# Two graph attention layers on one core: masks cleared ahead of their readers, counts last in a round

## The chip, the cores and the metric

The kernel runs on one core of a Trainium2 chip. The core has five engines that each work through a queue of their own, in order: TensorE (PE in the profile, with PEld for its weight loads), VectorE (DVE), ScalarE (ACT), GpSimd (POOL) and SyncE (SP). [...] The metric is the device time of one execution in microseconds. A measurement here is a median of several runs.

## What is computed

There are N = 3327 nodes with D = 1024 features each, and an adjacency matrix of 3327 x 3327 integers. Each pair is drawn with a chance of 0.0024 in either direction, the matrix is made symmetric, and every node is its own neighbour; a row then holds 17.1 ones on average. Two layers follow one another. Both are graph attention with a residual and a layer norm; layer 0 has 8 heads of 128 features, layer 1 has one head and a ReLU.

```python
# layer 0
h = (x @ W).reshape(C, H, D)
e = alpha_src[:, :, None] + alpha_dst[:, None, :]      # per head
e = jnp.where(e >= 0, e, NEG_SLOPE * e)
e = jnp.where(adj[None] == 0, -jnp.inf, e)
attn = jax.nn.softmax(e, axis=-1)
out = jnp.einsum('hij,hjd->hid', attn, h_heads)
x = _layernorm(x + out)
# layer 1: the same with one head, relu(attention @ h), and again a layer norm
```

## The kernel before

**Tiles and stages.** The nodes form 26 tiles of 128 rows (`NT`); the last one has 127. The program has three parts. The projection stage multiplies every tile of x with the weights of layer 0 on TensorE (`project`, line 538: a tile has three column groups c of 347, 347 and 346 columns, each a chain of 8 products in float32), writes h to memory (`keep`), and beside this makes the neighbour lists of all tiles. From tile 13 on it also sums the early half of the lists (`sums_so_far`, line 617; one small step of it at each pace call). Then one of two arms runs both layers: `sparse` (line 955), which gathers the listed rows of h by indirect DMA, or `by_pairs` (line 1373), which goes over all 26 x 26 pairs of tiles.

**Which arm runs** is decided on the chip. A tile's list holds, for each group of 32 rows and each half of the columns, 256 places (`HG2`); what does not fit goes to one more block of 128 places for the whole tile. `words` counts the neighbours of each row in each half, `ends` takes running sums of the counts within groups of 32 rows and keeps what lies over 256, and `ends2` takes the running sum of that over the tile, into `cnt[:, t, 3]`. A node's own entry is no part of the list: it is cleared from the mask first, and added from the diagonal later. At the end of the stage the largest of these numbers is compared with 128, and the result is read as the branch's condition:

```python
        nc.vector.tensor_copy(big[:, :, 1], cnt[:, :, 3])                                   # L900
        nc.vector.tensor_scalar(flag, most, float(P), None, op0=OP.is_gt)                   # L907
    with tc.If(dense > 0) as arm:                                                           # L1491
        with ExitStack() as own:
            by_pairs(own)
    with arm.Else():
        with ExitStack() as own:
            sparse(own)
```

**Masks.** A tile's 128 rows of the adjacency matrix are loaded from memory as bytes by a DMA that GpSimd issues (`load_mask`, line 524). There are three buffers, and tile t uses number t % 3 (line 526). `words` (line 335) has its own entry cleared by GpSimd (line 342), counts each half with two ScalarE instructions (line 346), and folds the mask into words with three VectorE instructions (line 353). `count(t)` (line 566) calls `words(t)` and then `load_mask(t + 2)`.

**The list work** is a generator, `listing` (line 572). A round has eight steps and serves two tiles, `new` = t + 1 (its entries are found) and `old` = t (its lists are put together on TensorE by `give` and read by `take` and `sources`). The steps of a round before the change: four with `keys` and `columns` on VectorE (with `ends(t + 3)` in the second and `ends2(t + 3)` in the fourth), then `take`, `ways` and `count(t + 4)`, then `sources`, then `places`, then `spread`.

**The order** is written out by hand (`tc.manual_schedule`), so each engine's queue is the order in which the Python code runs. `pace` (line 608) is called after every second product; it advances `listing` until its steps done are in proportion to the calls: `done * slots[1] >= slots[0] * 216`. `slots` starts at a number set by hand. Rounds for tiles 0 to 2 are partly written out before the loop (`count(0)` to `count(2)`, `ends`, `ends2`); the loop over t = 3 to 25 then holds two projections of tile t, one of t + 1, and the transposes of tile t + 2 (`flip`: four on TensorE into the one bank "T", copied out by ScalarE at line 199).

**The arm `by_pairs`** has no order by hand. For each tile it loads the adjacency rows again, from memory into one buffer `ad` in bfloat16, compares them with zero (line 1387), turns the 26 blocks on TensorE (line 1393), copies them to bytes and stores them. Layer 0 then takes 7 chunks of up to four tiles, 8 heads and 26 source tiles j: ScalarE forms e of 128 x 512 (Relu), VectorE adds and multiplies with the mask, and TensorE makes two products of it, of 128 x 512 with h (line 1448) and of 32 x 512 with a column of ones (line 1450). After each head the sums are copied, turned and added. `project1` (line 1401) makes 16 products of 128 x 512 for each tile, and layer 1 makes, for each of 26 tiles and 26 sources, three products of 341 or 342 columns (line 1485). It reads neither the lists nor the masks of the first stage.

Of the kernel before, what the change touches and what calls it, by code (L numbers as in the profile page):

```python
# [14 lines left out]
OP = mybir.AluOpType  # L15
# [4 lines left out]
P = 128  # L20
# [6 lines left out]
def kernel(  # L27
# [28 lines left out]
    nc = tc.nc  # L56
    N, D = x.shape
    H, DH = a0_src.shape
    NT = (N + P - 1) // P
# [35 lines left out]
    def rows(t):  # L95
        return min(P, N - t * P)
# [217 lines left out]
    class Edges:  # L314
# [10 lines left out]
        def factors(self):  # L325
# [6 lines left out]
            nc.gpsimd.tensor_copy(mv[:, 1, :], r[:, 1, :])  # L332
            nc.gpsimd.tensor_tensor(mv[:, 2, :], r[:, 1, :], mv[:, 1, :], OP.subtract)

        def words(self, ad, junk):

            sbuf, ph, t = self.ph.sbuf, self.ph, self.t  # L340
            own = ad[:, t * P : (t + 1) * P].bitcast(mybir.dt.int8)
            nc.gpsimd.affine_select(  # L342
                out=own, in_=own, pattern=[[1, P]], compare_op=OP.not_equal, fill=0.0, base=0, channel_multiplier=-1
            )
            for n in range(2):
                nc.scalar.activation(junk, ad[:, n * THR : (n + 1) * THR], AF.Copy, accum_out=self.d[:, n : n + 1])  # L346
            self.deg_b = sbuf("deg_b", [P, 2], 4, dt=BF16)
            nc.scalar.activation(self.deg_b, self.d, AF.Copy)
            w = ad.bitcast(I32)
            for n in range(3):  # L350
                m = WD >> n
                half = sbuf(f"wd{n}", [P, m], 4 if n == 2 else 1, dt=I32)
                nc.vector.scalar_tensor_tensor(
                    half, w[:, m:], 1 << n, w[:, :m], op0=OP.logical_shift_left, op1=OP.bitwise_or
                )
                w = half
            self.bytes = w.bitcast(U8)
# [152 lines left out]
    with ExitStack() as own, tc.manual_schedule():  # L510
        ph = Phase(own, "proj", {"A": 2, "T": 1})
# [4 lines left out]
        xts, xT, ads, hts, accs = {}, {}, {}, {}, {}  # L516
        lists = [Edges(ph, t) for t in range(NT)]
# [15 lines left out]
        def flip(t, g, who=None):  # L533
            if g == 0:
                xT[t] = ph.sbuf("xT", [P, KT, P], 2) if t else part.sbuf("z", [P, KT, P], 1, "xT")
            (who or ph).turned(xT[t], xts[t] if g == 0 else xts.pop(t), g)

        def project(t, c, paced=True, between=None):

            acc = accs[t, c] = bank("A", [P, CUTS0[c + 1] - CUTS0[c]], "mm")  # L540
            for k in range(KT):
                nc.tensor.matmul(  # L542
                    acc, xT[t][:, k, :], wt[:, k, CUTS0[c] : CUTS0[c + 1]], start=k == 0, stop=k == KT - 1
                )
                if k == 3 and between:
                    between()
                if paced and k % 2 == 1:
                    pace()

        def keep(t, c):  # L550
            if t not in hts:
                hts[t] = ph.sbuf("ht", [P, HW0], 3)
            ht, acc, c0 = hts[t], accs.pop((t, c)), CUTS0[c]
            m = min(CUTS0[c + 1], D) - c0
            if c == 2:
                nc.scalar.activation(sd0[:, t].rearrange("p a h -> p (a h)"), acc[:, m:], AF.Copy)
                lists[t].factors()
                nc.scalar.activation(ht[:, D : D + H], acc[:, m + H :], AF.Exp)
                nc.scalar.activation(ht[:, D + H :], acc[:, m + H :], AF.Exp, scale=SLOPE)
                scored.add(t)  # L560
            nc.scalar.activation(ht[:, c0 : c0 + m], acc[:, :m], AF.Copy)  # L561
            kept[t] = kept.get(t, 0) + 1
            if kept[t] == 3:
                nc.sync.dma_start(h0_d[t * P : (t + 1) * P, :HW0], hts.pop(t))

        def count(t):
            if t < NT:
                lists[t].words(ads.pop(t), junk)
                if t:
                    load_mask(t + 2)  # L570

        def listing():

            for t in range(-1, NT):
                old, new = lists[t] if t >= 0 else None, lists[t + 1] if t + 1 < NT else None
                for s in range(4):
                    if old and s:
                        old.give(s - 1)
                    if new:
                        (new.keys, new.columns)[s // 2](s % 2)  # L580
                    if s == 1 and 2 < t + 3 < NT:
                        lists[t + 3].ends(tri_b)
                    if s == 3 and 2 < t + 3 < NT:
                        lists[t + 3].ends2(all_b)
                    yield
                if old:
                    old.give(EB - 1)
                    old.give(EB)
                    old.take()
                if new:  # L590
                    new.ways()
                count(t + 4)
                yield
                if old:
                    old.sources()
                    yield
                while new and t + 1 not in scored:
                    yield
                if new:
                    new.places()  # L600
                    yield
                    new.spread()
                    yield

        scored, kept, soon = set(), {}, []
        steps, slots, done = listing(), [0, 0], [0]

        def pace():
# [202 lines left out]
        for g in range(NG):  # L811
            nc.vector.memset(tri[g * GT : (g + 1) * GT, g * GT : (g + 1) * GT], 1.0)
        nc.gpsimd.affine_select(
            out=tri, in_=tri, pattern=[[1, P]], compare_op=OP.is_ge, fill=0.0, base=0, channel_multiplier=-1
        )
        tri_b = pool.tile([P, P], BF16, bufs=1, name="tri_b")
# [6 lines left out]
        )  # L823
        all_b = pool.tile([P, P], BF16, bufs=1, name="all_b")
        nc.vector.tensor_copy(all_b, tri)
        count(0)
        for _ in range(2):
            next(steps)
# [8 lines left out]
        project(1, 2, False)  # L837
        keep(1, 2)
        lists[0].ends2(all_b)
        lists[1].ends(tri_b)  # L840
        flip(3, 0)
        load_x(5)
        count(2)

        done[0], slots[:] = 4, [9, (NT - 3) * 12 + 13]
        project(2, 2, True, lambda: flip(3, 1))
        keep(2, 2)
        flip(4, 0)
        lists[1].ends2(all_b)
        lists[2].ends(tri_b)  # L850
        project(3, 2, True, lambda: flip(4, 1))
        keep(3, 2)
        lists[2].ends2(all_b)
        for t in range(3, NT):
            load_x(t + 3)
            if 4 <= t < 4 + KT:
                nc.sync.dma_start(wt1[:, t - 4, :], w1[(t - 4) * P : (t - 3) * P, :])
            if t == 12:
                n, own_a = NT - 1, pool.tile([P, NT], I32, bufs=1, name="own")
                nc.vector.memset(own_a[:, n:], 0)  # L860
                step, m = adj.ap[0][0] + 1, rows(n)
                nc.sync.dma_start(
                    own_a[:, :n], bass.AP(tensor=adj.tensor, offset=adj.offset, ap=[[step, P], [P * step, n]])
                )
                nc.sync.dma_start(
                    own_a[:m, n:], bass.AP(tensor=adj.tensor, offset=adj.offset + n * P * step, ap=[[step, m], [1, 1]])
                )
            if t == 11:
                ph.iota([P, P], [[1, P]], "io_t", base=1, dst=io_t)
                same = ident[: NG * H, : NG * H].rearrange("p (g h) -> p g h", g=NG)  # L870
                met = meets.rearrange("p (g t) -> p g t", g=NG)
                nc.vector.tensor_reduce(met[:, :, 0], same, AX.X, OP.max)
                nc.vector.tensor_copy(met[:, :, 1:], met[:, :, :1].to_broadcast([NG * H, NG, GT - 1]))
                nc.vector.tensor_reduce(heads, same.rearrange("p g h -> p h g"), AX.X, OP.max)
            if t == 16:
                nc.gpsimd.tensor_copy(loop, own_a)
            if t in (9, 10):
                table, w = (h0_d, HW0) if t == 9 else (y_d, HW)
                blank = pool.tile([P, 1, HP - w], F32, bufs=1, name=f"blank{t}")
                nc.gpsimd.memset(blank, 0.0)  # L880
                nc.sync.dma_start(
                    table[:, w:].rearrange("(t p) w -> p t w", p=P), blank.to_broadcast([P, NT, HP - w])
                )
            if t == NTH:
                soon.append(sums_so_far())
            for c in (0, 1):
                project(t, c)
                keep(t, c)
            if t + 2 < NT:
                flip(t + 2, 0)  # L890
            if t + 1 < NT:
                project(t + 1, 2)
                keep(t + 1, 2)
            if t + 2 < NT:
                flip(t + 2, 1)
# [624 lines left out]
```

## Time and profile before

| what | number |
| --- | --- |
| median of 3 runs | 1940.33 us (1933.4 to 1942.73) |
| the profiled execution | 1945.79 us |
| its span, first to last instruction | 1944.1 us |
| busy: PE, DVE, ACT, POOL | 1633.7, 1184.5, 573.4, 1092.2 us |
| projection stage: first and last product of line 542 | 13.0 and 570.5 us |
| the flag is written (line 907) | 571.5 us |
| first instruction of the arm that ran (`sparse`) | 594.2 us |
| products of line 1267 (layer 1's projection, in `sparse`) | 1230.8 to 1935.4 us |

Times in the profile's rows are microseconds from the span's start; a duration printed as "mean ns" is in nanoseconds. A row of a timeline has the start, the length, the engine, the line, the operation, and how many instructions were merged into it; in square brackets is the time the engine stood idle before it and what ended that. A float32 product appears as two records, so 8 records are 4 products. The arm that ran is `sparse`; `by_pairs` has no row in this profile.

### The profile page before, as it was taken

To read this page: it belongs to the slowest core of one execution; us is meant where nothing else is said; L and a number is where in the kernel's file an instruction comes from. 1 tells how busy PE (TensorE), PEld (TensorE's weight loads), DVE (VectorE), ACT (ScalarE), POOL (GpSimd) and SP (SyncE) were. 2 spreads that over 40 slices of the span, in tenths; PEclk is the share of its full clock that TensorE was granted. 3 is DMA by queue.
4 is the path that set the end of the run, shared out by engine and by line. 5 is a ranking of instruction groups with operands and counts; after the bars stand their busy time and mean duration, and the time that the engine had idled before them with its cause. 6 is when DMAs were issued, how large, how long until landed. Compare 5 with 4: busy or idle time off the path is not lost.

```text
span 1944.1 us, 35431 instructions
## 1 busy us (share of the span) xinstructions
PE 1633.7 (84%) x13168; PEld 919.9 (47%) x13168; DVE 1184.5 (61%) x3261; ACT 573.4 (29%) x1565; POOL 1092.2 (56%) x1580
## 2 busy tenths in 40 slices
PE   8699989989994777777777665798989999899988
PEld 5466556655563554554455442243434434333433
DVE  6699988777765776777777774243444344434342
ACT  5656554444321222222222121022122221222121
POOL 4433346656555666666666555565656666565640
PEclk9899999999996878888878877899999999999999
DMA  6555779887779999999999998899999999899980
GB/s 178 91 130 114 144 152 293 255 249 238 247 271 349 381 391 393 383 393 371 402 386 386 374 313 301 310 374 340 346 350 369 335 394 342 331 362 340 325 302 33
DMA packets 183364, 585.16 MB, mean 301 GB/s; under 512 B 36168, under 2 KB 42824, under 8 KB 183182
## 3 DMA queue, kind: packets, MB, share of 16 engines
q0 software_dynamic: 131056, 457.74, 68.4%
q1 hardware_dynamic: 52126, 125.06, 17.2%
q8 instruction: 107, 1.75, 0.4%
q14 instruction: 75, 0.61, 0.1%
HBM read 586.09 MB, written 51.22 MB: 328 GB/s over the span
## 4 chain that ended last, share of the span: by engine, by line
PE 43%; issue 10%; DVE 6%; ACT 4%; DMA 4%; POOL 1%; another core or an unknown queue 0%; DVEq 0%; ACTq 0%; POOLq 0%
PE mm L1267 17%; PE acc L1235 13%; PE acc L1129 8%; PE acc L1110 2%; DMA src<-h_d,idx 2%; PE tr L196 1%; ACT L1193 1%; PE acc L1118 1%; DVE e L1098 1%; ACT own L1076 1%; DMA near<-h_d,idx 1%; DVE pr L982 1%; DVE st L217 1%; ACT L220 1%; DMA src<-y_d,idx 1%
## 5 line engine op out<-in xcount | busy, mean ns | idle before, releaser
L542 PE MATMUL mm<-wt,xT 128*128 128x347 f32 (+1 forms) x1248 | 416.6, 475 | 6.8 <-ACT ht L561 3.3
L1267 PE MATMUL mm<-wt,xT 128*128 128x512 f32 x832 | 395.5, 613 | 2.6 <-issue 2.3
L1017 POOL DMA_INDIRECT src<-y_d,idx x248 | 249.1, 1005 | 166.8 <-PE acc L1235 71.0
L542 PEld LDWEIGHTS mm<-wt,xT 128*128 128x128 f32 x1248 | 228.5, 195 | 118.3 <-issue 19.7
L1017 POOL DMA_INDIRECT src<-h_d,idx x184 | 196.5, 1068 | 121.3 <-PE acc L1129 35.8
L1267 PEld LDWEIGHTS mm<-wt,xT 128*128 128x128 f32 x832 | 152.3, 193 | 211.5 <-issue 206.7
L1270 DVE SCALAR_TENSOR_TENSOR o<-mm,y 128x512 f32<-128x512 f32 x52 | 36.0, 692 | 322.2 <-PE acc L1235 126.4
L1017 POOL DMA_INDIRECT near<-y_d,idx x168 | 169.5, 1009 | 108.7 <-PE acc L1235 48.3
L1129 PE MATMUL acc<-src,e 128*32 128x128 f32 x2944 | 161.3, 324 | 52.1 <-issue 47.5
L1017 POOL DMA_INDIRECT near<-h_d,idx x120 | 130.6, 1088 | 82.4 <-PE acc L1129 31.0
L1235 PE MATMUL acc<-src,es 128*32 128x341 f32 x1488 | 130.6, 485 | 41.8 <-DVE es L1226 31.8
L1129 PEld LDWEIGHTS acc<-src,e 128*32 128x32 f32 x2944 | 111.5, 130 | 113.4 <-issue 93.8
L1098 DVE TENSOR_TENSOR e<-oh,way 128x1024 f32<-128x1024 f32 x104 | 127.1, 1222 | 59.3 <-ACT w L1096 43.1
L1129 PE MATMUL acc<-near,e 128*32 128x128 f32 x2048 | 116.0, 333 | 48.7 <-issue 34.8
L199 ACT ACTIVATE xT<-tr 128x512 f32<-128x512 f32 x104 | 62.1, 598 | 299.9 <-PE tr L196 151.6
L1129 PEld LDWEIGHTS acc<-near,e 128*32 128x32 f32 x2048 | 79.7, 133 | 93.7 <-issue 84.4
L1096 ACT ACTIVATE w<-way 128x32 f32<-128x32 f32 x104 | 20.3, 195 | 351.4 <-DVE way L1094 186.6
L1249 ACT ACTIVATE z<-y,ri 128x342 f32<-128x342 f32 (+1 forms) x78 | 39.5, 569 | 277.0 <-issue 121.6
L1235 PE MATMUL acc<-near,es 128*32 128x342 f32 (+1 forms) x1008 | 85.8, 469 | 21.3 <-DVE es L1226 14.0
L629 POOL DMA_INDIRECT near<-h_d,idx x76 | 82.1, 1080 | 31.5 <-issue 22.9
L1235 PEld LDWEIGHTS acc<-src,es 128*32 128x32 f32 x1488 | 44.4, 114 | 115.0 <-issue 61.1
L346 ACT ACTIVATE junk<-ad 128x1664 uint8<-128x1664 uint8 x52 | 83.8, 1611 | 16.2 <-POOL ad L342 14.8
(242 smaller groups left out, 2587.8 us busy)
## 6 DMA issues: line engine op xcount, KB each, us to landing
h_d<-ht SPq DMA_DIRECT2D x26, 520.0 KB
own<-h_d SPq DMA_DIRECT2D x26, 520.0 KB
y_d<-y SPq DMA_DIRECT2D x26, 514.0 KB
y<-y_d SPq DMA_DIRECT2D x26, 514.0 KB
x<-in_x_dram SPq DMA_DIRECT2D x25, 512.0 KB
y<-in_x_dram SPq DMA_DIRECT2D x25, 512.0 KB
out_dram<-o SPq DMA_DIRECT2D x25, 512.0 KB
ad<-in_adj_dram POOLq DMA_DIRECT2D x25, 415.9 KB
```

The lines of the kernel that those rows point to most:

```text
L199: nc.scalar.activation(part, tr, AF.Copy)
L346: nc.scalar.activation(junk, ad[:, n * THR : (n + 1) * THR], AF.Copy, accum_out=self.d[:, n : n + 1])
L542: nc.tensor.matmul(acc, xT[t][:, k, :], wt[:, k, CUTS0[c] : CUTS0[c + 1]], start=k == 0, stop=k == KT - 1)
L629: nc.gpsimd.indirect_dma_start(out=src[n % 3][:, g, :], out_offset=None, in_=h0_d[:THR, :], in_offset=bass.IndirectOffsetOnAxis(ap=idx[:, ...
L1017: nc.gpsimd.indirect_dma_start(out=s[:, g, :w], out_offset=None, in_=table[:n, :], in_offset=bass.IndirectOffsetOnAxis(ap=idx[:, t, b * NG ...
L1098: nc.vector.tensor_tensor(e, oh.unsqueeze(2).to_broadcast([P, ng, H, wide]), wp.unsqueeze(3).to_broadcast([P, ng, H, wide]), OP.mult,)
L1110: nc.tensor.matmul(self.acc[j - 1].rearrange("p h d -> p (h d)"), ident, self.h[:, (j - 1) * HALF : j * HALF], start=False, stop=False,)
L1129: nc.tensor.matmul(self.acc[h // 4][g * GT : (g + 1) * GT, h % 4, :], e[:, g, h, :], rowsof[:, g, h, :], start=first and h % 4 == 0, stop= ...
L1235: nc.tensor.matmul(self.acc[c][to, :m], es[:, g, :], s[:, g, CUTS[c] : CUTS[c + 1]], start=b == 0, stop=b == EB,)
L1249: nc.scalar.activation(z[:, cut], self.res[:, cut], AF.Copy, scale=ri[:, 1:2])
L1267: nc.tensor.matmul(acc, xT[:, k, :], wt1[:, k, half], start=k == 0, stop=k == KT - 1)
L1270: nc.vector.scalar_tensor_tensor(o[:, half], acc, 0.0, res[:, half], op0=OP.max, op1=OP.add)
```

## The change

Four things change, all in the first stage. `words` no longer clears the mask; a new `clear` does, and is called for tiles 0 to 2 ahead of everything and for tile t + 4 in the third step of round t. `count(t + 4)` moves from the fifth step of a round to a last step of its own, and `places` and `spread` become one step, so a round still has eight. Ahead of the loop, `slots` starts at 4 of 284 instead of 9 of 289; `lists[1].ends` comes after the transposes of tile 3; and `count(2)` and `lists[1].ends2` come after the first paced projection, `project(2, 2)`. One projection of tile 3 moves from the loop to a place ahead of it, between `lists[2].ends` and `lists[2].ends2`.

```diff
+        def clear(self, ad):
+            own = ad[:, self.t * P : (self.t + 1) * P].bitcast(mybir.dt.int8)
+            nc.gpsimd.affine_select(
+                out=own, in_=own, pattern=[[1, P]], compare_op=OP.not_equal, fill=0.0, base=0, channel_multiplier=-1
+            )
         def words(self, ad, junk):
-            own = ad[:, t * P : (t + 1) * P].bitcast(mybir.dt.int8)
-            nc.gpsimd.affine_select(
...
+        def clear(t):
+            if t < NT and t not in cleared:
+                cleared.add(t)
+                lists[t].clear(ads[t])
         def count(t):
             if t < NT:
+                clear(t)
                 lists[t].words(ads.pop(t), junk)
                 if t:
                     load_mask(t + 2)
@@ listing
+                    if s == 2 and t >= 0:
+                        clear(t + 4)
...
                 if new:
                     new.ways()
-                count(t + 4)
                 yield
...
                 if new:
                     new.places()
-                    yield
                     new.spread()
                     yield
+                count(t + 4)
+                yield
@@ ahead of the loop
+        for t in range(3):
+            clear(t)
         count(0)
...
         lists[0].ends2(all_b)
-        lists[1].ends(tri_b)
         flip(3, 0)
         load_x(5)
-        count(2)
-        done[0], slots[:] = 4, [9, (NT - 3) * 12 + 13]
+        lists[1].ends(tri_b)
+        done[0], slots[:] = 4, [4, (NT - 3) * 12 + 8]
         project(2, 2, True, lambda: flip(3, 1))
         keep(2, 2)
+        lists[1].ends2(all_b)
+        count(2)
         flip(4, 0)
-        lists[1].ends2(all_b)
-        lists[2].ends(tri_b)
         project(3, 2, True, lambda: flip(4, 1))
         keep(3, 2)
+        lists[2].ends(tri_b)
+        project(3, 0)
+        keep(3, 0)
         lists[2].ends2(all_b)
@@ loop
-            for c in (0, 1):
+            for c in (0, 1)[t == 3 :]:
                 project(t, c)
```

More of the change, by code (lines that the diff above doesn't have):

```diff
@@ L333, in factors @@
             nc.gpsimd.tensor_tensor(mv[:, 2, :], r[:, 1, :], mv[:, 1, :], OP.subtract)
-        def words(self, ad, junk):
-            sbuf, ph, t = self.ph.sbuf, self.ph, self.t
-            own = ad[:, t * P : (t + 1) * P].bitcast(mybir.dt.int8)
+        def clear(self, ad):
+            own = ad[:, self.t * P : (self.t + 1) * P].bitcast(mybir.dt.int8)
             nc.gpsimd.affine_select(
@@ L344, in words @@
             )
+        def words(self, ad, junk):
+            sbuf = self.ph.sbuf
             for n in range(2):
@@ L600, in listing @@
                     new.places()
-                    yield
                     new.spread()
                     yield
-        scored, kept, soon = set(), {}, []
+                count(t + 4)
+                yield
+        scored, cleared, kept, soon = set(), set(), {}, []
         steps, slots, done = listing(), [0, 0], [0]
```

## The prediction

> **What bounds the kernel now.** I read the stage boundaries first, then the waits of the stage that the change touches. In VectorE's timeline the flag that selects the arm is written at 571 us, and the arm's first instruction runs at 594 us:
>
> ```profile
> 571.46 0.14 DVE L907 TENSOR_SCALAR flag<-most 1x1 int32<-1x1 f32 x1
> 594.24 0.12 DVE L965 MEMSET y<- 128x4 f32 x3 [6.06 <-DMA half_d<-z]
> ```
>
> So everything the edit moves lies in the first 30% of the span. There TensorE is the nearly full engine. Its timeline shows the gaps that the change aims at (line 362 waits behind ScalarE, which waits for a clear; line 466 waits for `spread`), and what a gap costs afterwards: eight records of line 542 take 4.18 us after a gap, where the same eight took 2.57 us at 87.93.
>
> ```profile
> 64.14 0.16 PE L362 MATMUL dd<-deg_b,tri_b 128*128 128x2 bf16 x1 [4.52 <-ACT cnt L388]
> 64.24 0.63 PE L196 MATMUL tr<-ident,x 128*128 128x128 f32 x4
> 64.70 4.18 PE L542 MATMUL mm<-wt,xT 128*128 128x346 f32 x8
> 78.66 0.48 PE L466 MATMUL xp<-mvg,place 128*128 128x168 bf16 x3 [9.34 <-ACT mvg L447]
> 79.01 3.98 PE L542 MATMUL mm<-wt,xT 128*128 128x346 f32 x8
> ```
>
> The table of waits up to 600 us (total, times, longest) shows the other target, VectorE waiting for the clear:
>
> ```profile
> DVE wd L353 <- POOL ad L342: 57.0, 13, 6.9
> ```
>
> **The change, part by part: first, which arm runs.** This decides everything, and it is a matter of order, not of duration. Before, `count(2)` stood ahead of `project(2, 2)`. Now it stands behind, and `project(2, 2)` makes four pace calls, with slots 5, 6, 7, 8 of 284. After 4 steps done, the condition 4 x 284 < 6 x 216 releases step 5 (`ways`), 5 x 284 < 7 x 216 step 6 (`places`, `spread`), and 6 x 284 = 1704 < 8 x 216 = 1728 step 7, the round's new last step: `count(3)`. `count(3)` ends with `load_mask(5)`, and 5 % 3 = 2: that is tile 2's buffer, which `count(2)` has not read yet. The queues of the built program agree: ScalarE has tile 3's two counts ahead of tile 2's, and tile 2's wait for the fifth mask load issued, tile 5's. So tile 2's list is made of tile 5's rows; that is the part of the computation which changes. Tile 2's clear ran on the old contents, and tile 5's comes a round later, so these rows are counted with their own entries.
>
> I summed the reference's adjacency matrix as `words`, `ends` and `ends2` do. With cleared masks the number compared with 128 is between 5 and 115 over the 26 tiles (tile 5: 47). Tile 5's rows uncleared gain 32 entries in the first half of each group: groups of 301, 294, 282 and 294 against 256 places give 147, and 10 + 12 from the second half make 169. 169 > 128, the flag is 1, and `by_pairs` runs both layers over all pairs. It has no row in this profile, so it is built up from the nearest rows.
>
> *A, up to the arm.* Removed: gaps of 4.52 + 9.34 us, another of 0.88 at 84.5, and 1.6 + 1.4 us of slow products after them: -17.7. Added: tile 2's counts wait for the new load. A mask load issued at 90.40 keeps the DMA engines busy until about 97.5 (share 0.94, then 0.20): 7.1 us.
>
> ```profile
> 91.00:97.00 6.00, 6.00 (x25) 3.80 (x24) 5.66 (x19) 5.70 (x17) 2.03 (x9) 1.00 0.94 149
> 97.00:98.00 1.00, 1.00 (x8) 0.59 (x6) 0.97 (x2) 0.00 (x0) 0.84 (x5) 1.00 0.20 20
> ```
>
> Tile 3's load is issued at 59.3 and lands at 66.4; its clear takes 0.3; tile 5's load then lands at 73.8; the two counts take 3.6 (59.62 to 63.2 before), to 77.4. Behind them in ScalarE's queue is the copy of tile 4's first transposes (0.6), and TensorE's second transposes of tile 4 need that bank. TensorE gets there at about 69.1 and waits until 78.0, 8.9 us, plus 1.6 slow: +10.5. Later TensorE waits behind VectorE's late clears (releasers of lines 435, 447 and 650 between 350 and 500 us: 4.83 + 2.33 + 1.73 + 0.99 + 0.65 + 0.54): -11.1. The clears' DMAs lead by 11 steps instead of 16, over 20 us against 7.1. Counts late in the round leave line 362 two steps instead of five; ScalarE's 3.6 us fit in two steps of about 1.9 us only just, so this gain can vanish. Arm at 594 - 17.7 + 10.5 - 11.1 = 576 (565 to 605: more hidden, or no gain at all).
>
> *B, loading the masks again*, one buffer, so a chain per tile: 7.1 load + 2.6 compare (line 224's 0.812 us for 1024 elements, times 3328/1024) + 4.0 until the last transposes (eight at 0.15, two copies of 1024 from PSUM at twice line 1270's 0.692) + 0.3 handed over = 14.0; 26 x 14.0 = 364. Ends: 11.5 (compare and copies at half) and 18 (the load writes two bytes instead of one): 300 to 470.
>
> *C, layer 0.* The rows for the two products of 512 columns, for ScalarE's 128 x 512 and for VectorE's:
>
> ```profile
> 1714.47 3.70 PE L1267 MATMUL mm<-wt,xT 128*128 128x512 f32 x8
> 1718.01 1.89 PE L1235 MATMUL acc<-end,es 128*128 128x341 f32 x6
> 1719.73 3.60 PE L1267 MATMUL mm<-wt,xT 128*128 128x512 f32 x8
> 1723.26 1.93 PE L1235 MATMUL acc<-src,es 128*32 128x341 f32 x24
> L199 ACT ACTIVATE xT<-tr 128x512 f32<-128x512 f32 x104 | 62.1, 598 | 299.9 <-PE tr L196 151.6
> L1270 DVE SCALAR_TENSOR_TENSOR o<-mm,y 128x512 f32<-128x512 f32 x52 | 36.0, 692 | 322.2 <-PE acc L1235 126.4
> ```
>
> Four products go from 1714.47 to 1718.01: 0.885 us each. Two of them per source, 1.77 us, exceed ScalarE's 0.60 and VectorE's 0.69, so TensorE sets the pace: 52 x 0.885 = 46.0 per head. At a head's end a chain stands open: two copies 1.2, transposes of the sums 0.6, of the next row 0.6, Exp 0.6, Relu 0.6, mask 0.7, handovers 0.4, together 4.7, and 1.6 of slow products after it as above: 52.3. 48 heads x 52.3 = 2510; the last chunk has half the width, 8 x 28.8 = 230; layer norms hold VectorE up 2 us in each chunk, 14. Sum 2754. Ends: 0.86 per product and no open chain, 44.7 x 48 + 22.4 x 8 = 2325; the mean of line 1267 over its busy time, 395.5/416 = 0.95, and a chain of 10 us, 3120.
>
> [...]
>
> *D, `project1`:* 16 x 0.885 + eight transposes 1.2 + a copy 0.6 + 0.1 = 16.1, x 26 = 419 (390 without the transposes and half the copy; 500 with the 3 us of scoring in series).
> *E, layer 1:* six records of line 1235 take 1.72 us up to the next row, 0.573 per product; 78 x 0.573 + 0.4 = 45.1, x 26 = 1173 (1160 to 1250). ScalarE and VectorE have a quarter of C's width against 1.72 us.
> *F, tail:* norm and store, 10.
>
> Sum: 576 + 364 + 2754 + 419 + 1173 + 10 = 5296, and 1.7 around the span: 5298. The profiled execution is 5 us above the median, less than this sum can tell; I take **5300 us**.
>
> **The rivals.** *The list arm still runs.* For it: the edits remove real gaps, as costed. Against it: the queue order and 169 > 128. It decides if tile 2's number stays at 128 or below. Time: 1945.8 - 17.7 + 10.5 - 11.1 = 1927, faster by 0.7% than the median. Chance 0.05. *The 32-column products cost next to nothing in `by_pairs`.* For it: 24 records of 128 x 32 take 1.93 us, hardly more than six of 128 x 128. Against it: those go in fours to different columns, here each stands alone between two full ones. Time: layer 0 falls to 48 x (23.0 + 6.3) + 8 x 17.3 + 14 = 1559, total 4103. Chance 0.07. *ScalarE, VectorE and TensorE take turns* because e is too scarce: 0.6 + 0.69 + 1.77 + 0.3 = 3.4 per source, layer 0 at 48 x 95 + 8 x 51 = 4970, total 7500. Against it: e has four buffers. Chance 0.06.
>
> **How the numbers follow.** The forecast, `by_pairs` bound by TensorE, has 0.80; 0.02 is left for others. The ends of A to F add up to 4750 and 5955 if all fall on one side; 4850 to 5850 leaves their corners and the rivals out, about 0.2. A measurement of this kernel can tell 0.5% from no change. Faster 0.05 (the first rival), same 0.01, slower 0.94.
>
> **What would show it.** Rows of `by_pairs` at all, and none of `sparse`; tile 2's counts on ScalarE behind tile 3's, with an idle time ended by a DMA; some 7.1 us or more from load to load in B; pairs of 512-column products 1.77 us apart with a gap near 5 us every 26 pairs. The forecast falls if the profile has line 1129's successor in it.

## The result, and the profile after

The changed kernel takes 5737.44 us (median of 6 runs, 5734.51 to 5743.24), the kernel before 1941.53 us on the same chip (6 runs, 1927.85 to 1953.39). The ratio is 2.957, with a 95% interval of 2.945 to 2.970: slower. The profiled execution has a span of 5741.5 us.

The page of the changed kernel shows which arm ran. First the shares of the chain that ended last by engine, then the costliest groups (busy us and mean ns of one; idle time before it and what ended that):

```profile
PE 85%; DVE 6%; DMA 5%; ACT 3%; issue 1%; POOL 0%; SPq 0%; another core or an unknown queue 0%; DVEq 0%; POOLq 0%; ACTq 0%
L1458 ACT ACTIVATE e<-R,nb,a 128x512 f32<-128x512 f32 (+1 forms) x1456 | 1120.7, 780 | 1881.5 <-PE sum L1465 1879.6
L1459 DVE SCALAR_TENSOR_TENSOR e<-e,b,pen 128x512 f32<-128x512 f32 (+1 forms) x1456 | 1030.0, 712 | 1593.5 <-ACT e L1458 1587.4
L1465 PE MATMUL sum<-e,ones 128*32 128x512 f32 (+1 forms) x2912 | 1479.8, 591 | 0.0
L1462 PE MATMUL acc<-e,h 128*128 128x512 f32 (+1 forms) x2016 | 1073.0, 614 | 0.0
L1462 PE MATMUL acc<-e,near 128*128 128x512 f32 (+1 forms) x896 | 556.6, 708 | 140.5 <-DVE e L1459 140.5
```

All these lines are `by_pairs`: the flag came out as 1. Of these three groups of TensorE two have no idle time before them; the third, the first eight sources of each head, has 140.5 us, at the heads' boundaries. ScalarE waits 1879.6 us for TensorE, so TensorE sets the pace, as forecast. Cut at the first and last instruction of each part (for the arm, VectorE's first), the span is:

| part | forecast us | measured us | from, to |
| --- | --- | --- | --- |
| A, up to the arm | 576 | 583.6 | 0 to 583.6 |
| B, masks again | 364 | 387 | to 971 |
| C, layer 0 | 2754 | 3191 | to 4162 |
| D, `project1` | 419 | 399 | to 4561 |
| E, layer 1 | 1173 | 1169 | to 5730 |
| F, tail | 10 | 12 | to 5742 |

The cause that A names is in ScalarE's timeline. Tile 3 is counted first (70.40), behind GpSimd's clear; tile 2's counts follow at 77.26, and what ends their wait is a DMA into a mask buffer, tile 5's rows. Line 199, the copy of turned x, stands behind them:

```profile
70.40 1.59 ACT L349 ACTIVATE junk<-ad 128x1664 uint8<-128x1664 uint8 x1 [2.23 <-POOL ad L338]
...
77.26 1.59 ACT L349 ACTIVATE junk<-ad 128x1664 uint8<-128x1664 uint8 x1 [2.39 <-DMA ad<-in_adj_dram]
...
80.79 0.58 ACT L199 ACTIVATE xT<-tr 128x512 f32<-128x512 f32 x1
```

TensorE's timeline has the wait that this makes, 10.99 us against a forecast of 8.9; the four transposes after it take 1.12 us instead of 0.63:

```profile
67.94 2.49 PE L545 MATMUL mm<-wt,xT 128*128 128x346 f32 x8
81.43 1.12 PE L196 MATMUL tr<-ident,x 128*128 128x128 f32 x4 [10.99 <-ACT xT L199]
```

Part B is a chain of load, compare, transposes and copies, one tile at a time, as forecast. In VectorE's timeline a tile is 13.94 us here (803.07 to 817.01), 14.6 on the mean of all:

```profile
803.07 1.03 DVE L1402 TENSOR_SCALAR ad<-ad 128x3328 bf16<-128x3328 bf16 x1 [8.02 <-DMA ad<-in_adj_dram]
805.22 3.88 DVE L1409 CAST pen<-mt 128x1024 uint8<-128x1024 bf16 x4 [1.13 <-PE mt L1408]
809.06 0.06 DVE L164 MEMSET ad<- 128x1 bf16 x1
817.01 1.03 DVE L1402 TENSOR_SCALAR ad<-ad 128x3328 bf16<-128x3328 bf16 x1 [7.89 <-DMA ad<-in_adj_dram]
```

Part C holds most of what the sum missed. TensorE's timeline, the last products of a head and the first of the next:

```profile
1994.29 1.05 PE L1465 MATMUL sum<-e,ones 128*32 128x512 f32 x2
1995.27 1.13 PE L1462 MATMUL acc<-e,h 128*128 128x512 f32 x2
1996.32 1.04 PE L1465 MATMUL sum<-e,ones 128*32 128x512 f32 x2
1998.04 1.05 PE L1471 MATMUL rs<-part,so 32*128 32x1 f32 x8 [0.68 <-ACT so L1467]
1999.02 0.66 PE L1476 MATMUL tr<-ident,ot 128*128 128x128 f32 x4
1999.52 0.60 PE L235 MATMUL tr<-ident,sd 128*128 128x128 f32 x4
2002.43 2.08 PE L1462 MATMUL acc<-e,near 128*128 128x512 f32 x2 [2.32 <-DVE e L1459]
2004.44 1.91 PE L1465 MATMUL sum<-e,ones 128*32 128x512 f32 x2
2006.28 2.08 PE L1462 MATMUL acc<-e,near 128*128 128x512 f32 x2
2008.29 1.17 PE L1465 MATMUL sum<-e,ones 128*32 128x512 f32 x2
2009.39 1.12 PE L1462 MATMUL acc<-e,near 128*128 128x512 f32 x2
```

A pair starts every 2.03 us (1994.29 to 1996.32), not every 1.77. From the end of the last pair (1996.32 + 0.98) to the next head 5.1 us pass, forecast 4.7. The first two pairs then take 3.85 and 3.11 us, so 2.9 us are lost to the slow clock, forecast 1.6. The windows of the same trace show that clock (after the busy times of PE, PEld, DVE, ACT and POOL: granted clock, DMA share, GB/s):

```profile
1997.00:2000.00 3.00, 2.32 (x17) 1.82 (x16) 0.46 (x3) 1.90 (x3) 0.00 (x0) 1.00 0.00 0
2000.00:2002.40 2.40, 0.12 (x2) 0.00 (x0) 1.61 (x6) 2.21 (x4) 0.00 (x0) 0.86 0.00 0
2002.40:2004.40 2.00, 1.97 (x2) 0.50 (x2) 2.00 (x3) 1.31 (x2) 0.00 (x0) 0.50 0.00 0
2004.40:2006.30 1.90, 1.90 (x4) 0.20 (x3) 0.10 (x1) 0.00 (x0) 0.00 (x0) 0.50 0.00 0
2006.30:2008.30 2.00, 2.00 (x4) 0.49 (x3) 0.75 (x1) 0.81 (x1) 0.00 (x0) 0.50 0.00 0
```

### The profile page after: what moved, and what is told of

It reads as the page before. It is cut to its first block, busy times and chain, and to the rows that moved or that the text cites. A ratio compares the mean times of both kernels' runs of the same rounds, so it can differ in the third digit from the quotient of the medians.

```text
span 5741.5 us, 44587 instructions
## 1 busy us (share of the span) xinstructions
PE 5185.7 (90%) x16103; PEld 2113.0 (37%) x16103; DVE 2150.5 (37%) x4322; ACT 2020.4 (35%) x3622; POOL 312.7 (5%) x861
## 4 chain that ended last, share of the span: by engine, by line
PE 85%; DVE 6%; DMA 5%; ACT 3%; issue 1%; POOL 0%; SPq 0%; another core or an unknown queue 0%; DVEq 0%; POOLq 0%; ACTq 0%
PE acc L1462 27%; PE sum L1465 24%; PE acc L1499 20%; PE mm L1425 6%; PE mm L545 4%; DMA ad<-in_adj_dram 4%; DVE pen L1409 2%; PE rs L1471 1%; PE part L670 1%; DMA near<-h_d,idx 1%; DVE e L1459 1%; ACT e L1458 1%; ACT so L1467 1%; PE tr L1476 1%; ACT R L237 0%
## 5 line engine op out<-in xcount | busy, mean ns | idle before, releaser
L1458 ACT ACTIVATE e<-R,nb,a 128x512 f32<-128x512 f32 (+1 forms) x1456 | 1120.7, 780 | 1881.5 <-PE sum L1465 1879.6
L1459 DVE SCALAR_TENSOR_TENSOR e<-e,b,pen 128x512 f32<-128x512 f32 (+1 forms) x1456 | 1030.0, 712 | 1593.5 <-ACT e L1458 1587.4
L1465 PE MATMUL sum<-e,ones 128*32 128x512 f32 (+1 forms) x2912 | 1479.8, 591 | 0.0
L1462 PE MATMUL acc<-e,h 128*128 128x512 f32 (+1 forms) x2016 | 1073.0, 614 | 0.0
L1499 PE MATMUL acc<-h,e 128*128 128x342 f32 (+1 forms) x2808 | 814.1, 450 | 0.0
L1462 PE MATMUL acc<-e,near 128*128 128x512 f32 (+1 forms) x896 | 556.6, 708 | 140.5 <-DVE e L1459 140.5
L1499 PEld LDWEIGHTS acc<-h,e 128*128 128x128 f32 x2808 | 530.7, 190 | 274.0
L1496 ACT ACTIVATE e<-R,nb,a 128x128 f32<-128x128 f32 x676 | 332.4, 492 | 729.8 <-PE acc L1499 729.8
L1462 PEld LDWEIGHTS acc<-e,h 128*128 128x128 f32 x2016 | 299.7, 188 | 783.8 <-DVE e L1459 644.0
L1499 PE MATMUL acc<-near,e 128*128 128x342 f32 (+1 forms) x1248 | 363.1, 450 | 0.9 <-DVE e L1497 0.9
```

Of the source, the lines that this page charges most:

```text
L1458: nc.scalar.activation(e, r, AF.Relu, bias=r0.nb[:, j, hd : hd + 1], scale=r0.a[:, j, hd : hd + 1])
L1459: nc.vector.scalar_tensor_tensor(e, e, r0.b[:, j, hd : hd + 1], pens[j // NTH][:, :nt, j % NTH, :], op0=OP.add, op1=OP.mult)
L1462: nc.tensor.matmul(acc[:, :w], hs[j][:, hd * DH : (hd + 1) * DH], e, start=j == 0, stop=j == NT - 1)
L1465: nc.tensor.matmul(total[:GR, :w], ones, e, start=j == 0, stop=j == NT - 1)
L1496: nc.scalar.activation(e, self.r[:, 0, :], AF.Relu, bias=r1.nb[:, j, :], scale=r1.a[:, j, :])
L1499: nc.tensor.matmul(self.acc[g][:, : CUTS[g + 1] - CUTS[g]], e, hs[j][:, CUTS[g] : CUTS[g + 1]], start=j == 0, stop=j == NT - 1,)
```

## The experiments

The chips of the runs differ: the kernel before took 1831 us on the first and third chip below and 1966 us on the second, so list-arm kernels are told as ratios to the runs of before beside them. The arm over all pairs hardly depends on the chip (its length is 5157.9 us in the changed kernel and 5155.7 in `before_pairs`, on two chips), so kernels that run it are compared by the arm's length: span less the time of VectorE's first instruction in the arm.

**Is the overtaken count the whole cause?** `load_after` keeps the change and only issues tile 5's load behind tile 2's count:

```diff
-                if t:
+                if t and t != 3:
                     load_mask(t + 2)
...
         count(2)
+        load_mask(5)
```

> The changed kernel with one move: the load of tile 5's mask is issued behind the counts of tile 2, which read the same buffer; the counts themselves stay where the change put them. Theory (the early load puts tile 5's rows into tile 2's list, and the number of 169 against 128 selects the arm over all pairs): the list arm runs again, no row of by_pairs in the trace, tile 2's counts no longer wait for a DMA, and the time is that of the first rival without the new wait, about 1941 - 17.7 - 11.1, so 1905 to 1930. Rival (the arm is chosen for another reason, or the late counts are slow by themselves): near 5737, or above 1941.

Measured: 1809.24 us (1808.15 to 1810.47), ratio 0.9876 (0.9859 to 0.9892); the expected 1905 to 1930 us are ratios of 0.981 to 0.994. The list arm runs; VectorE's timeline has its first instruction there:

```profile
562.84 0.12 DVE L981 MEMSET y<- 128x4 f32 x3 [8.58 <-DMA half_d<-z]
```

Moving one DMA issue behind the count that it overtook takes away all of the slowdown, and what is left of the change is a gain of 1.2%. The flag has a second input, four times the largest number of neighbours of a row (line 898, just ahead of the copy of `cnt[:, :, 3]`, which is line 899). In tile 5's uncleared rows that is 4 x 29 = 116, under 128, so it isn't what set the flag.

**What would the change be worth if the flag were ignored?** `after_lists` is the changed kernel with a higher bound:

```diff
-        nc.vector.tensor_scalar(flag, most, float(P), None, op0=OP.is_gt)
+        nc.vector.tensor_scalar(flag, most, 1024.0, None, op0=OP.is_gt)
```

> The changed kernel with the flag's threshold at 1024 instead of 128, so that the list arm runs with the list that the change makes; tile 2's list holds tile 5's rows, and what exceeds the 128 places of its extra block is left out. Theory: the first rival of the prediction, 1927 by its sum; in the changed kernel's trace the arm began 10.6 us earlier than before, so 1925 to 1935. It stands above the run with the later load by the wait for that load, some 10 us (11.0 idle before line 196 in the changed kernel's trace) or less. Rival (order alone costs time): 1941 or more.

Measured: 1809.4 us (1807.85 to 1810.18), ratio 0.9876 (0.9859 to 0.9892), equal to `load_after`; the expected 1925 to 1935 us, ratios of 0.992 to 0.997, were too high. TensorE's wait behind the late reload is 10.87 us here. In `load_after` a wait is still there, because tile 3's count, ahead of tile 2's, waits for its own clear (2.00 us, at 69.92). TensorE's timeline of `load_after`:

```profile
78.45 1.11 PE L196 MATMUL tr<-ident,x 128*128 128x128 f32 x4 [8.26 <-ACT xT L199]
```

The 2.6 us between the two waits do not reach the end.

**Is the arm by itself the added time?** `before_pairs` is the kernel before, made to take the other arm:

```diff
-        nc.vector.tensor_scalar(flag, most, float(P), None, op0=OP.is_gt)
+        nc.vector.tensor_scalar(flag, most, -1.0, None, op0=OP.is_gt)
```

> The kernel before with the flag's threshold at -1, so that the arm over all pairs always runs; its first stage is untouched. Theory (the arm is all of the added time): the changed kernel's 5737 plus the 10.6 us by which its arm began earlier, 5735 to 5760, with the same 2.03 us per pair of products and 14.6 us per tile in the mask stage. Rival (the change slows the arm too, by what it leaves in buffers or queues): clearly under 5700.

Measured: 5744.14 us, arm 5155.7 us, 3.14 times the kernel before beside it. The other arm alone triples the time, with the first stage untouched.

**Why does a pair of products take 2.03 us?** `wide_ones` is the changed kernel with the column of ones 128 wide instead of 32, so that every product of the pair has the same shape:

```diff
-        ones = pool.tile([P, GR], F32, name="ones")
+        ones = pool.tile([P, P], F32, name="ones")
...
-                    nc.tensor.matmul(total[:GR, :w], ones, e, start=j == 0, stop=j == NT - 1)
+                    nc.tensor.matmul(total[:, :w], ones, e, start=j == 0, stop=j == NT - 1)
```

> The changed kernel with a block of 128 columns of ones in place of 32 in layer 0 of by_pairs, so that both products of a pair are 128 x 128; the extra sums are not read. Theory (alternating 128 x 128 with 128 x 32 costs 0.13 us per product): the pair falls from 2.03 to 1.77 us, layer 0 by 0.26 x 1248 + 0.13 x 208, about 350 us, to 5390. Rival 1 (the pair is bound by weight loads or by the alternation of two accumulators): 2.03 us stays, 5737. Rival 2 (a wider stationary block takes longer to load and that shows): over 5737.

Measured: 5257.2 us (5255.73 to 5258.67). Its arm takes 4693.0 us, 463 less than in `before_pairs` (about 350 expected). In TensorE's timeline the pairs now start 1.716 us apart (1935.03 to 1936.74), and each product takes the same:

```profile
1935.03 1.02 PE L1465 MATMUL sum<-e,ones 128*128 128x512 f32 x2
1935.88 1.02 PE L1462 MATMUL acc<-e,h 128*128 128x512 f32 x2
1936.74 1.02 PE L1465 MATMUL sum<-e,ones 128*128 128x512 f32 x2
1937.60 1.02 PE L1462 MATMUL acc<-e,h 128*128 128x512 f32 x2
```

The weights to be loaded are four times as wide and the pair is still 0.314 us shorter: 0.157 us on the mean for each of its two changes of shape, and 0.858 us for a product that follows one like it. Two rival readings fall: that a narrow product is cheap, and that wider weights make the pair longer. A third, that a narrow product takes longer for each column, is settled by the last chunk, whose products have 256 columns. In TensorE's timeline of the changed kernel a pair there takes 1.178 us (mean of 16):

```profile
4138.33 0.62 PE L1465 MATMUL sum<-e,ones 128*32 128x256 f32 x2
4138.88 0.70 PE L1462 MATMUL acc<-e,h 128*128 128x256 f32 x2
4139.51 0.62 PE L1465 MATMUL sum<-e,ones 128*32 128x256 f32 x2
```

In that of `wide_ones` it takes 0.864 us (mean of 8):

```profile
3573.28 0.59 PE L1465 MATMUL sum<-e,ones 128*128 128x256 f32 x2
3573.72 0.59 PE L1462 MATMUL acc<-e,near 128*128 128x256 f32 x2
3574.15 0.59 PE L1465 MATMUL sum<-e,ones 128*128 128x256 f32 x2
```

The difference is 0.314 us again, so it is a price for each pair and not for each column. The expectation had priced the half-width pairs at 0.13 us.

**Is the boundary of a head the next head's row?** `row_ahead` is the changed kernel, with that row made in the middle of the head before:

```diff
+            ahead = {}
             for hd in range(H):
-                r = ph.row(r0, range(t0, t0 + nt), hd)
+                r = ahead.pop(hd) if hd else ph.row(r0, range(t0, t0 + nt), hd)
                 acc, total = bank("A", [P, CW], "acc"), bank("S", [P, CW], "sum")
                 for j in range(NT):
+                    if j == NTH and hd + 1 < H:
+                        ahead[hd + 1] = ph.row(r0, range(t0, t0 + nt), hd + 1)
```

> The changed kernel, in layer 0 of the arm over all pairs the next head's row is turned and laid out at source 13 of the head before, not behind its end. The prediction's chain at a head's end is 4.7 us (5.1 measured), of which transposes of the row 0.6, Exp 0.6, Relu 0.6, mask 0.7 would leave it, and part of 2.9 us of slow products behind it: 49 boundaries x 2.5 to 5.4 = 120 to 265 us, time 0.954 to 0.979 of the changed kernel's. Rival (the boundary is set by the copies and the addition of the head before, not by the row): 0.995 to 1.000.

Measured: 5478.38 us (2 runs), arm 4891.7 us, 266 less than the changed kernel's, a shade beyond the upper end: 5.4 us for each of 49 boundaries. In its timeline the boundary has no idle time at all. The pair across it takes 3.60 us (1973.62 to 1977.22), and the 1.56 us over 2.03 are the closing work of the head before (1974.68 to 1976.24):

```profile
1973.62 1.13 PE L1465 MATMUL acc<-e,near 128*128 128x512 f32 x2
1974.68 1.05 PE L1474 MATMUL rs<-part,so 32*128 32x1 f32 x8
1975.66 0.66 PE L1479 MATMUL tr<-ident,ot 128*128 128x128 f32 x4
1976.24 1.05 PE L1468 MATMUL sum<-e,ones 128*32 128x512 f32 x2
1977.22 1.13 PE L1465 MATMUL acc<-e,near 128*128 128x512 f32 x2
```

The first product of the next head is even ahead of the last head's closing work, and the granted clock from 1000 to 3900 us is 0.99, against 0.95 in layer 0 of the changed kernel.

**Which part of the change gains in the list arm?** Three kernels, first on the slower chip. `count2_ahead` is the changed kernel with tile 2 counted where nothing can overtake it:

```diff
         lists[1].ends(tri_b)
+        count(2)
...
         lists[1].ends2(all_b)
-        count(2)
```

> The change with count(2) ahead of project(2, 2) again, behind lists[1].ends; all else as in the change. Tile 5's load can no longer overtake tile 2's count, so the list arm must run. Theory (TensorE's gap behind the late reload is absorbed later by a VectorE-bound stretch): the ratio to the kernel before is that of the kernel that only issues tile 5's load late, 0.9876, within 0.003. Rival (the first stage is still TensorE's, so removing what is left of the wait behind ScalarE, 8.3 us there, is worth it): 0.983 to 0.984.

`count_mid` is that, with `count(t + 4)` back in the fifth step and `places` and `spread` separate again:

```diff
                 if new:
                     new.ways()
+                count(t + 4)
                 yield
...
                     new.places()
+                    yield
                     new.spread()
                     yield
-                count(t + 4)
-                yield
```

> As the kernel with count(2) ahead, but count(t + 4) back in the fifth step of a round and places and spread two steps again; of the change only the early clear and part of the order by hand are left. Theory A (counts late in the round make TensorE wait at line 365 for ScalarE, some 13.6 us in eight waits in the run that loads tile 5 late, and these count): 0.980 to 0.983. Theory B (VectorE sets the pace there, so the waits cost nothing): equal to the kernel with count(2) ahead within 0.002. The prediction's own sentence, that this gain can vanish, is A.

`clear_only` is the kernel before, with the new `clear` and its calls and nothing else of the change:

> The kernel before with the early clear alone: tiles 0 to 2 up front, tile t + 4 in the third step of a round; counts, slots and the hand-written order as before. By the prediction's terms VectorE's 57 us behind clears go, and 11.1 us of TensorE's waits behind them: ratio 0.994, arm of the lists. If the clear is the whole of the gain: 0.9876. If the hand-written order is the whole of it: 0.998 to 1.000.

Measured there: `count2_ahead` 0.9805 (0.9759 to 0.9851), `count_mid` 0.9799 (0.9756 to 0.9843), `clear_only` 0.9916 (0.9883 to 0.9949). On that chip the clear alone is 1.2% slower than `count_mid`, and their runs don't overlap (1936 to 1959 us against 1920 to 1930). But their first stages end alike: the flag is written at 553.0 and 552.7 us, and the arm begins at 574.3 and 575.4 us. So the difference lies in the list arm, whose code the two share; its cause wasn't found. The three were taken once more on a chip on which the runs of before spread less (0.4% instead of 1.7%), with a profile of the kernel before from the same chip:

> The kernel before itself, one profile on the chip that the next three runs use, so that the stage of the projections can be compared row by row. Flag at 571.5 us in the first profile; between 560 and 575 here.

> The early clear alone once more, on a chip shared with the next two. Theory (the clear ends the first stage some 18 us earlier, which the first profile's flag at 553.0 suggests): flag 15 to 20 us ahead of the kernel before's on this chip, ratio 0.989 to 0.992.

> Counts late in a round, count(2) ahead of project(2, 2), once more. Its first profile had the flag at 562.6, 10 us behind the one with counts in mid-round. Theory A (late counts cost the first stage): flag 8 to 12 us later than in the next kernel, ratio 0.004 to 0.006 above it. Theory B: within 3 us and 0.002.

> Early clear, order by hand as changed, counts in mid-round, once more. If the hand-written order is worth anything beyond the clear, below the kernel with the clear alone by 0.003 or more; if not, equal to it within 0.002. Best of the four by theory A above.

| kernel, third chip | median us | ratio, 95% interval | flag us | arm's first instruction us |
| --- | --- | --- | --- | --- |
| before (9 runs; flag and arm from one more) | 1831.24 | | 568.0 | 589.6 |
| early clear alone | 1803.54 | 0.9859 (0.9839 to 0.9879) | 537.5 | 558.7 |
| changed, count(2) ahead | 1802.25 | 0.9846 (0.9832 to 0.9860) | 538.8 | 559.6 |
| the same, counts in mid-round | 1805.24 | 0.9856 (0.9839 to 0.9872) | 539.4 | 561.5 |

All three are faster than the kernel before, and here the early clear alone gains as much as any; the extra 1.2% of the second chip isn't there. The flag is 30.5 us earlier with it (expected 15 to 20), and the end 27.7 us. The tables of waits (total, times, longest) over the first 580 us show what it removes. In the kernel before:

```profile
DVE wd L353 <- POOL ad L342: 56.9, 13, 7.0
```

With the early clear alone:

```profile
DVE wd L356 <- POOL ad L338: 13.0, 4, 6.5
```

VectorE's 56.9 us behind clears have become 13.0. Some 8 us of the lead are made in the first 82 us, where TensorE's gap of 4.52 us at line 362 shrinks to 1.04 (line 365 there): the eight records that stand at 89.59 us in the kernel before start at 81.53. The windows show where the rest is made, with the same columns as above. The kernel before:

```profile
100.00:300.00 200.00, 185.42 (x893) 121.47 (x892) 182.09 (x522) 115.68 (x369) 80.23 (x327) 0.98 0.65 145
300.00:500.00 200.00, 180.36 (x1658) 118.56 (x1657) 154.18 (x420) 94.80 (x290) 119.72 (x266) 0.97 0.83 252
```

The early clear alone:

```profile
100.00:300.00 200.00, 185.39 (x943) 122.11 (x941) 182.36 (x523) 118.07 (x373) 83.25 (x315) 0.97 0.68 156
300.00:500.00 200.00, 196.69 (x1875) 131.17 (x1876) 166.24 (x457) 97.18 (x307) 138.40 (x296) 0.99 0.88 278
```

Between 100 and 300 us TensorE and VectorE are as busy in both; between 300 and 500, where the gathers and sums of the early half run beside the projection, TensorE is busy for 16.3 us more. The hand-written order trades one early gap of TensorE for another and gains nothing that can be told on this chip: with the clear alone line 469 still waits 9.24 us for ScalarE, and with `count(2)` ahead that gap is gone, but there is a wait of 4.9 us at line 196 and one of 14.4 us in eleven parts behind the late counts. TensorE's timeline with the clear alone:

```profile
71.75 0.48 PE L469 MATMUL xp<-mvg,place 128*128 128x168 bf16 x3 [9.24 <-ACT mvg L450]
```

TensorE's table of waits with `count(2)` ahead:

```profile
PE dd L365 <- ACT deg_b L351: 14.4, 11, 3.1
```

Theory A of the late counts falls: the flags are 0.6 us apart and the ratios 0.0010, and on the slower chip the medians were 1923.71 and 1922.44. The flag of the first profile of `count2_ahead`, 10 us later, didn't come again; that was the slowest of its six runs. `count2_ahead` itself came out between its two forecasts on the third chip (0.9846) and below both on the second (0.9805), so whether the rest of the wait behind ScalarE is worth anything stays open.

## Why the prediction was right, and where it was off

**Which arm.** Right, and for the reason given: the four pace calls release `count(3)` and tile 5's load ahead of tile 2's count, and the two runs that touch only that load and only the flag's bound separate it cleanly. That the number is 169 comes from summing the matrix; the runs show only that it lies above 128 and not above 1024. The first rival, that the list arm still runs (1927 us), gave the right kind of time for a kernel without the overtaking: 0.993 of the median before against 0.985 to 0.988 measured on the faster chips.

**A.** 7.6 us too small. The wait was 10.99 us and not 8.9: tile 3's load is issued at 61.57 us and not at 59.3, and its clear starts at 70.07, 8.5 us later where the sum had 7.1. Nor is most of that wait the reload's, as the sum had it: `load_after`, without the reload ahead of the counts, still waits 8.26 us, because tile 2's counts now stand behind tile 3's. What was also wrong is the step that split the gain: -17.7 for early gaps through the hand-written order and -11.1 through the clears. The clear alone moved the arm's start by 30.9 us on the third chip, and the order by nothing that can be told there. In the changed kernel the arm starts 10.6 us before that of the first profile of before; on the chip of `after_lists` it starts at 562.4 us against 586.6 for `before_pairs`, 24 us earlier. Why the chip of the result gains less wasn't settled.

**B.** 387 for 364 us, near by terms that in part cancel. VectorE waits 8.5 us on the mean for a load (220.1 us over 26), where the sum had 7.1 and 0.3; the compare takes 1.03 and not 2.6; and from the compare to the end of the copies 5.0 us pass (1.13 + 3.88) and not 4.0. The sum let the next load start behind the last transposes. It starts behind the last copy, because it waits for line 164, which clears the buffer's last column and stands in VectorE's queue behind the copies (809.06): its issue on GpSimd, line 166, waits for that 24 times, 339.7 us in all. The price of the compare was scaled from a float32 row of another line, 0.79 ns an element; this bfloat16 one takes 0.31.

**C.** This is the mis-sized term, 3191 for 2754 us, in the step that took the price of a product from the rows of line 1267. A chunk of eight heads takes 484.7 us (from the first head's end at 1028.64 to the next chunk's at 1513.35), so six take 2908 where the sum had 6 x (8 x 52.3 + 2) = 2522. Of these 386 us, 48 x 26 x (2.03 - 1.77) = 324 are the pairs, and the rest, 1.3 us a head on the mean, the boundaries; the last chunk, at half width, holds some 51 more. Of the 0.157 us per change that `wide_ones` shows, the price holds 0.027 (0.885 - 0.858); what in a change takes the time, no run here separates. The two groups in the prediction's rows couldn't tell, because each holds one change: four products take 3.54 us ahead of a 128 x 128 row (1714.47 to 1718.01) and 3.53 ahead of a 128 x 32 row (1719.73 to 1723.26). The change of the first group is ahead of it: at 1714.47 it comes itself right behind a 128 x 32 row of the kernel before, which I left out of my reading.

```profile
1712.61 1.93 PE L1235 MATMUL acc<-src,es 128*32 128x341 f32 x24 [1.28 <-DVE es L1226]
```

And I took the mean of four products with a change among them, 0.885, as the price of a product, where 0.858 is the product's own. The rival that a narrow product costs next to nothing was wrong in the other direction: it takes 0.98 us from start to start (1994.29 to 1995.27), where the wide one in its place takes 0.858 in `wide_ones`.

**The boundary.** The sum of the chain was near (5.1 for 4.7 us), in part by luck: the four one-column products of line 1471 (eight records), 0.98 us until the next transposes start, weren't in it, and one of its two copies runs beside the last product (1996.43). The slow products behind it were mis-sized, 2.9 for 1.6 us. The price came from a gap in the first stage, after which eight records took 1.6 us too long; here the granted clock stays at 0.50 from 2002.40 to 2008.30, 5.9 us, of which half is lost. Not every boundary costs as much: from head to head within a chunk the changed kernel takes 59.5 to 60.9 us. In windows of 0.2 us the granted clock here is 1.00 up to 2001.60 and 0.50 from 2001.80. That is 1.6 us after the last transpose and 4.4 us after the last product of 512 columns. No run here separates which of the two the fall goes with, or shows why it comes then.

**D, E, F.** Off by -20, -4 and +2 us. In the rival in which three engines take turns, e would have been scarce; instead ScalarE waits 1879.6 us for TensorE, as the groups of the profile's page show.

## What to carry to other kernels

When a reader of a buffer is moved, look for the write that takes the buffer next and count the calls that release it: a scheduler by shares can let the write overtake. A wrong input may not show as a wait, but as a branch that runs something else, so work out what the data do, not only the times. Price a change of product shape between neighbours by itself: 0.157 us twice in every pair was 9% of the arm here (463 of 5155.7 us), and in `wide_ones` padding the narrow operand to 128 columns removed it.

## What the hardware showed that was not expected

A narrower stationary operand made the program slower: the product with 32 columns of ones cost more than one with 128, because of its neighbours (2.03 against 1.716 us a pair).

A gap of 5.1 us without products of 512 columns cost 2.9 us more after its end, and a few instructions moved ahead removed the idle time and the slow clock: 5.4 us a boundary in `row_ahead`.

The kernel before, which runs the list arm, differs by 7% between chips (1831 and 1966 us); the arm over all pairs takes 5157.9 us on one chip and 5155.7 on another, 0.04% apart.
